# Turning the rows of routings 1 to 5 through DRAM and VectorE instead of TensorE

## The chip, the cores and the metric

The kernel runs on one core of a Trainium2 chip. The metric is the device time of one execution in microseconds (us). A core has these engines, each with its own in-order instruction queue: PE (TensorE, matrix products and transposes by an identity matrix, into PSUM), DVE (VectorE), ACT (ScalarE), POOL (GpSimd) and SP (SyncE, which here only issues transfers). Transfers run on 16 DMA engines. An engine waits at the head of its own queue until what it needs is there, and all that stands behind it waits too.

## The reference, cut to what matters

```python
x = x + scan_layer(layernorm(x), ...)            # "attn_a": 8 batches, 512 tokens, 256 features
x = x + ffn(layernorm(x), ...)                   # 16 routed experts, 4 per token, and 2 shared ones
x = x + attention(layernorm(x), ...)             # "attn_b"
x = x + ffn(layernorm(x), ...)

# in ffn, for each token row x of the normalised input:
scores = sigmoid(x @ router_w.T)                 # 16 experts
s = scores + bias
group_score = top_k(s by groups of 4, 2).sum()   # 4 groups, the best 2 are kept
topk_idx = top_k(masked s, 4)
tw = 2.5 * scores[topk_idx] / sum(scores[topk_idx])
routed = sum over the 4 chosen experts of tw * (silu(x @ gate) * (x @ up)) @ down
shared = (silu(x @ sh_gate) * (x @ sh_up)) @ sh_down
```

For the products with the router and the shared experts' weights, the 512 normalised rows of a batch (tokens on the partitions) have to be turned, so that the features lie on the partitions. This turning is what the change is about.

## The kernel before, in words

All arithmetic is in float32. Tokens are handled in 8 batches of 512. The program has four stages: the scan stage (scan layer of all batches, routing of the first mixture and its shared experts), the blocks of 128 tokens sorted by expert (the first mixture's routed experts), the attention stage with the routing and the shared experts of the second mixture, and the second mixture's blocks. The change touches the scan stage, which ends near 330 us.

`stretch(layer)` writes a stage. Its loop over the batch `b` makes one list of pieces of work for each turn and issues them beside each other: in the turn of batch `b` there are the scan of batch `b` (`main`: the products `pz_s` at L563, the scan itself on DVE, the output product `py_s` at L510), the normalisation of batch `b+1` with its turning (`xn`, `pt_l`) and the load of that batch's `x` (L149), the routing of batch `b-1` (class `Route`), and a share of the shared experts' work of earlier batches (`pg_m` at L1146, `pd_m` at L1174). `timed(steps, *places)` gives each step of a piece its place as a fraction of the turn. A scheduler then orders the instructions of each engine by these places and by what they need, and the order stays fixed in each engine's queue.

The routing of a batch has these steps. `norm` writes the normalised rows `sorted_m` on DVE (L493) at the places `norms`. `scores` turns them, then multiplies with the router (`logits`: 8 small products `pl_m`, L669), turns the small result on DVE (L680) and takes the sigmoid on ACT. `choices` picks the experts on DVE (L695 to L739); the product `pr_m` (L747) counts places early in the next turn; the rows are then scattered to DRAM by POOL (L798).

There are two ways to turn. `turned` (from L416) makes 8 PE transposes of 128x128 into two PSUM banks (L430) and two copies of 128x512 out of them (L432). For the routings of batches 0 to 5 in the scan stage both copies are ACT's and go into a place kept free in `w_all` (`kept_rows`), from which the shared experts read later. `by_shares` (from L435) stores the rows in DRAM (L440, 512 KB), loads them back in four shares of 128 KB, each of runs of 64 floats (L443), and then turns 32x32 blocks by two DVE transposes of 128x512 (L452). Before the change it is used in the attention stage only: `r.scores(i == 1)` at L1543.

What sets the order on the SP queue: in each turn the store of `x` of the batch before (L1444), then the load of the next `x` (L149), and directly behind it, by `Scan.load`, the loads of two experts' weights (in the turns of batches 2 to 5 six of 256 KB, L235 to L237) and one block of zeros (L348 or L351). The pool for `x` has three buffers, so the load of the next `x` waits until DVE has written the `sorted_m` rows that are read from the buffer to be reused. The stores of the shared experts' sums (`ys_m`, L1184) are also on SP. The tag `kb4` is a ring of 9 buffers of 512 KB, which also holds `xn`, the scan's `y_s`, the shared experts' `act_m` and `ys_m`.

Of the kernel before, what the change touches and what calls it, by code (L numbers as in the profile page):

```python
# [19 lines left out]
NT = T // P  # L20
# [62 lines left out]
def tile_hybrid_block(  # L83
# [276 lines left out]
    def behind(*pieces):  # L360
        def steps():
            for piece in pieces:
                yield from piece.steps

        return Piece(sum(piece.columns for piece in pieces), steps())

    def beside(*pieces):


        def steps():  # L370
            done = dict.fromkeys(range(len(pieces)), 0)
            while done:
                k = min(done, key=lambda k: done[k] / pieces[k].columns)
                step = next(pieces[k].steps, None)
                if step is None:
                    del done[k]
                else:
                    done[k] += step
                    yield step

        return Piece(sum(piece.columns for piece in pieces), steps())

    def timed(steps, *places):


        def scaled():
            now = 0
            for place in places:
                yield place - now
                now = place  # L390
                next(steps)
            for _ in steps:
                pass

        return Piece(1, scaled())

    def spread(first: float, last: float, many: int):
        return [first + (last - first) * k / many for k in range(many)]

    def some(steps, many: int):  # L400

        for _ in range(many):
            yield next(steps)

    def issue(piece):
        for _ in piece.steps:
            pass
# [114 lines left out]
    class Scan:  # L522
# [3 lines left out]
        early = 0  # L526


        norms, scores, choose = (0.08, 0.2, 0.32, 0.4), (0.53, 0.57, 0.65, 0.69), (0.71, 0.97)
        last_rows, last_scores = (0.26, 0.33), (0.43, 0.46)  # L530

        def load(self, b: int):
# [667 lines left out]
    class Attention:  # L1200
# [4 lines left out]
        norms, scores, choose = (0.0, 0.12, 0.2, 0.28), (0.29, 0.45, 0.55, 0.6), (0.66, 0.95)  # L1205
# [215 lines left out]
    def stretch(layer):  # L1421


        i = layer.mixture
        xT, xn, made, routes, sends = {}, {}, {}, {}, []

        def norm(b: int, first: bool = False):
            def place():
                xn[b] = kb4(f"xn_{i}_{b}")
                return xn[b]  # L1430

            return normed(b, f"l{i}_{b}", place, False, first)

        def turn(b: int, copies=layer.copies):
            if i == 1 and b >= layer.ahead:
                return by_shares(lambda: xn.pop(b), f"l{i}_{b}", lambda xnT: xT.update({b: xnT}), True)
            return turned(lambda: xn.pop(b), f"l{i}_{b}", lambda xnT: xT.update({b: xnT}), copies)

        def project(b: int):
            made[b], piece = layer.project(b, xT.pop(b))  # L1440
            return piece
# [12 lines left out]
        def experts(many: int):  # L1454
            return Piece(many * each, some(whole, many))
# [39 lines left out]
        def start_route(b: int):  # L1495
            routes[b] = Route(i, b, layer.copies)
            store(b)
            return routes[b]
# [4 lines left out]
        for b in range(1 if begun else 0, B):  # L1503
            pieces = [begun or layer.main(b, made.pop(b))]
            begun = None
            nxt, last = b + layer.ahead, b == B - 1
            scores, choose, turns = layer.scores, layer.choose, layer.turns
            if i == 0 and b == 1:

                scores, choose, turns = (0.95, 0.955, 0.97, 0.975), (0.98, 0.99), (0.96, 0.965)  # L1510
            fill = []
            if layer.ahead > 1 and not last:
                fill.append(project(b + 1))
            if b > 1:
                shared_sum = experts(layer.quota[last])
                fill.append(shared_sum)
                if len(sends) > 1:
                    pieces.append(timed(sends.pop(0), *spread(0.0, 0.16, layer.over)))
                wait = 0.16 if i == 0 and b == 2 else 0.0
                first = [wait + place for place in (0.1, 0.14, 0.18)]  # L1520
                if layer.over:
                    pieces.append(timed(some(sends[0], 3 + NT * TK - layer.over), *first, *spread(0.22 + wait, 0.97, NT * TK - layer.over)))
                else:
                    pieces.append(timed(sends.pop(), *first, *spread(0.22, 0.66 if last else 0.86, NT * TK)))
            if fill:
                pieces.append(behind(*fill))
            if b > 0:
                r = start_route(b - 1)
                if last:
                    pieces.append(timed(r.norm(), *spread(0.0, 0.12, NT), *spread(*layer.last_rows, NT)))  # L1530
                else:
                    first, then, rows, full = layer.norms
                    pieces.append(timed(r.norm(), *spread(first, then, NT), *spread(rows, full, NT)))
                sends.append(r.rest)
                if last:
                    pieces += [
                        timed(r.scores(), *layer.last_scores, *spread(0.5, 0.56, NT)),
                        timed(some(r.rest, PICKS), *spread(0.57, 0.67, PICKS - 1), 0.76),
                        timed(some(r.rest, 3 + layer.sent), 0.79, 0.81, 0.83, *spread(0.85, 1.0, layer.sent)),
                    ]  # L1540
                else:
                    pieces += [
                        timed(r.scores(i == 1), *scores[:2], *spread(*scores[2:], NT)),  # L1543
                        timed(some(r.rest, PICKS), *spread(*choose, PICKS)),
                    ]
            if nxt < B:
                added = layer.load(nxt)
                if added is not None:
                    pieces.append(timed(added, 0.31, 0.34))
                stats = 0.36 if added is not None else 0.32  # L1550
                pieces += [
                    timed(norm(nxt), *spread(stats, 0.44, NT), *spread(0.56, 0.64, NT)),
                    timed(turn(nxt), *turns),
                ]
            issue(beside(*pieces))
            if layer.ahead == 1 and nxt < B:
                issue(project(nxt))
            if i == 0 and b == 2:
                for make in pending:
                    make()  # L1560
# [4 lines left out]
        r = start_route(B - 1)  # L1565
# [24 lines left out]
    with banks_of(one=8):  # L1590
        table = stretch(Scan())
        wqkv_sb, wo_sb = load_attention_weights()
# [6 lines left out]
    with banks_of(one=4, pair=2):  # L1599
        table = stretch(Attention())  # L1600
# [87 lines left out]
```

## Time and profile before

| what | value |
|---|---|
| median of 13 runs | 1616.82 us (1613.52 to 1619.73) |
| the profiled execution: its own time | 1614.3 us |
| its span, first to last instruction | 1612.6 us |
| PE busy, share of the span | 1569.6 us (97%) |
| DVE, ACT, POOL busy | 1002.7, 780.1, 772.8 us |
| mean granted PE clock | 0.99 of full speed |
| turns of batches 2, 3, 4, 5, 6 in the scan stage start at | 49.7, 88.2, 122.2, 156.3, 190.4 us |
| the turn of batch 7 starts at | 226.1 us |
| a PE transpose `pt_m`, and an ACT copy out of it | 282 ns and 591 ns (medians) |
| a DVE transpose of `by_shares` (attention stage) | 700 ns (median of 12) |

A turn starts with the first `pz_s` product of its batch. The times of PE instructions overlap, since matmuls are pipelined: the step from one start to the next is what a group costs. So the 8 transposes `pt_m` at 105.80 are shown as 1.10 us, but the next product starts 0.94 us after them.

The views used are the page, the timelines of single engines (start, duration, engine, line, operation, output and inputs, count, and in brackets the idle time before it and what ended it), and tables by window of time (start:end, length, then busy time and count of PE, PE's weight loads, DVE, ACT and POOL, then the granted PE clock, the busy share of the DMA engines and GB/s). "SPq" is the SP queue issuing transfers.

### The profile page before, as it was taken

To read this page: it belongs to the slowest core of one execution; us is meant where nothing else is said; L and a number is where in the kernel's file an instruction comes from. 1 tells how busy PE (TensorE), PEld (TensorE's weight loads), DVE (VectorE), ACT (ScalarE), POOL (GpSimd) and SP (SyncE) were. 2 spreads that over 40 slices of the span, in tenths; PEclk is the share of its full clock that TensorE was granted. 3 is DMA by queue.
4 is the path that set the end of the run, shared out by engine and by line. 5 is a ranking of instruction groups with operands and counts; after the bars stand their busy time and mean duration, and the time that the engine had idled before them with its cause. 6 is when DMAs were issued, how large, how long until landed. Compare 5 with 4: busy or idle time off the path is not lost. (4 is left out here: it accounts for less than half of the span.)

```text
span 1612.6 us, 34092 instructions
## 1 busy us (share of the span) xinstructions
PE 1569.6 (97%) x10030; PEld 1158.2 (72%) x10030; DVE 1002.7 (62%) x3264; ACT 780.1 (48%) x1622; POOL 772.8 (48%) x639
## 2 busy tenths in 40 slices
PE   8999999999999999999999999999999999999996
PEld 6566666589999999983444454544558999999996
DVE  6887765344467444437888988878744444544453
ACT  3344443245555555546544554454224555555553
POOL 4376665535556555550014432433533555555554
PEclk9999999999999999999999999999999999999998
DMA  5454424557777666641323433343745767777776
GB/s 172 138 193 153 147 101 142 174 98 104 124 124 109 100 100 96 91 68 41 87 82 101 140 97 116 101 123 99 276 147 93 107 114 127 118 138 134 136 136 135
DMA packets 282765, 196.88 MB, mean 122 GB/s; under 512 B 168688, under 2 KB 262672, under 8 KB 282576
## 3 DMA queue, kind: packets, MB, share of 16 engines
q1 hardware_dynamic: 230016, 121.50, 28.8%
q0 software_dynamic: 51984, 72.09, 24.8%
q8 instruction: 85, 1.39, 0.4%
q10 hardware_dynamic: 576, 1.05, 0.2%
q14 instruction: 104, 0.85, 0.2%
HBM read 91.29 MB, written 103.23 MB: 121 GB/s over the span
## 5 line engine op out<-in xcount | busy, mean ns | idle before, releaser
L1073 POOL DMA_INDIRECT part<-rows x272 | 426.6, 1568 | 341.3 <-ACT rows L1072 251.8
L798 POOL DMA_INDIRECT xg<-sorted_m,slots_m x256 | 269.1, 1051 | 244.7 <-ACT slots_m L795 119.2
L1033 PEld LDWEIGHTS ph<-rows,gate 128*128 128x128 f32 x2160 | 277.6, 191 | 32.7 <-ACT rows L1016 22.6
L1033 PE MATMUL ph<-rows,gate 128*128 128x128 f32 x2160 | 291.7, 278 | 0.5 <-ACT rows L1016 0.5
L1033 PE MATMUL ph<-rows,up 128*128 128x128 f32 x2160 | 285.3, 275 | 0.0
L1063 PE MATMUL pyr<-w_all,rows 128*128 x1088 | 279.5, 380 | 1.4 <-DVE rows L1043 1.4
L1033 PEld LDWEIGHTS ph<-rows,up 128*128 128x128 f32 x2160 | 262.9, 192 | 0.0
L1006 DVE COPY up<-w_all 128x512 f32 x270 | 119.2, 442 | 226.3 <-PE ph L1033 211.5
L1006 ACT COPY gate<-w_all 128x512 f32 x270 | 166.4, 617 | 123.9 <-PE ph L1033 120.0
L1043 DVE TENSOR_TENSOR rows<-ph,rows 128x256 f32<-128x256 f32 x272 | 115.5, 425 | 155.8 <-PE ph L1033 141.9
L1295 ACT ACTIVATE w_all<-ps_a 128x1024 f32<-128x1024 f32 x160 | 155.2, 1021 | 107.0 <-PE ps_a L1285 102.2
L1063 PEld LDWEIGHTS pyr<-w_all,rows 128*128 128x128 f32 x1088 | 186.8, 192 | 15.8 <-DVE rows L1043 1.6
L1072 ACT ACTIVATE rows<-pyr,gain 128x256 f32<-128x256 f32 x272 | 128.9, 474 | 78.5 <-PE pyr L1063 61.7
L1041 ACT ACTIVATE rows<-ph 128x256 f32<-128x256 f32 x272 | 104.6, 384 | 117.0 <-PE ph L1033 106.7
L1174 PE MATMUL pd_m<-sd_sb,act_m 128*128 128x256 f32 x512 | 120.1, 384 | 2.2 <-DVE act_m L1165 1.3
L1174 PEld LDWEIGHTS pd_m<-sd_sb,act_m 128*128 128x128 f32 x512 | 96.3, 191 | 26.6 <-issue 9.0
L1285 PE MATMUL ps_a<-w_all 32*128 32x384 f32 (+3 forms) x1024 | 103.5, 470 | 9.8 <-ACT w_all L1295 9.7
L1305 DVE SCALAR_TENSOR_TENSOR w_all<-w_all,causal 128x512 f32<-128x512 f32 (+1 forms) x160 | 91.9, 574 | 27.9 <-ACT w_all L1295 26.8
L1146 PE MATMUL pg_m<-w_all,su_sb 128*128 128x512 f32 x192 | 92.7, 606 | 0.0
L1146 PE MATMUL pg_m<-w_all,sg_sb 128*128 128x512 f32 x192 | 92.2, 601 | 0.0
L1285 PEld LDWEIGHTS ps_a<-w_all 32*128 32x128 f32 x1024 | 44.9, 186 | 65.0 <-ACT w_all L1295 36.4
L1321 PE MATMUL po_a<-w_all,v_a 128*32 128x512 f32 (+3 forms) x1024 | 90.0, 449 | 0.0
(222 smaller groups left out, 1918.4 us busy)
## 6 DMA issues: line engine op xcount, KB each, us to landing
rows<-xg SPq DMA_DIRECT2D x720, 32.0 KB
rows<-xg SPq DMA_DIRECT2D x92, 134.0 KB
part<-x SPq DMA_DIRECT2D x16, 512.0 KB
w_all<-in_L_ffn_gate_w_dram SPq DMA_DIRECT2D x29, 256.0 KB
w_all<-in_L_ffn_up_w_dram SPq DMA_DIRECT2D x29, 256.0 KB
w_all<-in_L_ffn_down_w_dram SPq DMA_DIRECT2D x29, 256.0 KB
part<-ys_m SPq DMA_DIRECT2D x14, 512.0 KB
sum<-part SPq DMA_DIRECT2D x14, 512.0 KB
```

The costliest lines, as they stand in the source:

```text
L798: nc.gpsimd.indirect_dma_start(out=xg[i], out_offset=bass.IndirectOffsetOnAxis(ap=slots[:, at : at + 1], axis=0), in_=rows[:, t, :], in_of ...
L1006: copy(here, w_all[:, bass.ds(held[n][0] + half * KD * F, KD * F)])
L1033: nc.tensor.matmul(ph[s][:, f * P : (f + 1) * P], lhsT=both[s][:, k * F + f * P : k * F + (f + 1) * P], rhs=rows[:, ROW + k * P : ROW + (k ...
L1041: nc.scalar.activation(act, ph[0], AF.Silu)
L1043: made = nc.vector.tensor_mul(act, ph[1], act)
L1063: nc.tensor.matmul(py, lhsT=act[:, f * P : (f + 1) * P], rhs=w_all[:, bass.ds(w + 2 * KD * F + f * D, D)], start=(f == 0), stop=(f == KF - 1),
L1072: nc.scalar.mul(y, py, gain[:, TK : TK + 1])
L1073: acc = nc.gpsimd.indirect_dma_start(out=parts[i][n % 2], out_offset=bass.IndirectOffsetOnAxis(ap=rows[:, D + 2 * TK : D + 2 * TK + 1].bit ...
L1146: made = nc.tensor.matmul(dst, lhsT=w[:, k, f * P : (f + 1) * P], rhs=xnT[:, k, :], start=(k == 0), stop=(k == KD - 1),)
L1174: nc.tensor.matmul(py[:, j, :], lhsT=acts[n][:, f, t * P : (t + 1) * P], rhs=shared[n][3][:, f, :], start=(n == 0 and f == 0), stop=(n == ...
L1285: nc.tensor.matmul(ps[j // 2][:, j % 2, col : col + n], lhsT=k_sb[w][r, o, c * P : (c + 1) * P], rhs=q_sb[r, o, c * P : T], start=True, st ...
L1295: nc.scalar.activation(es[two], ps[two], AF.Exp, scale=ATT_SCALE)
```

## The change

The routings of batches 1 to 5 in the scan stage use `by_shares` instead of `turned`; batch 0 and the last two keep `turned`. (In the loop, `b` is the batch of the scan, and the routing is that of batch `b-1`; the turn `b = 7` has a call of its own.) The places of the routing steps in these turns move as well: the first step of `scores` (the store and the four loads) to 0.42 of the turn, the second (the DVE transposes) to 0.64, the router's product to 0.69 to 0.73, and the choice of the experts from 0.71 to 0.97 to 0.75 to 0.98.

```diff
-        norms, scores, choose = (0.08, 0.2, 0.32, 0.4), (0.53, 0.57, 0.65, 0.69), (0.71, 0.97)
+        norms, scores, choose = (0.08, 0.2, 0.32, 0.4), (0.42, 0.64, 0.69, 0.73), (0.75, 0.98)
...
-                        timed(r.scores(i == 1), *scores[:2], *spread(*scores[2:], NT)),
+                        timed(r.scores(i == 1 or b > 1), *scores[:2], *spread(*scores[2:], NT)),
```

The function that these routings now go through:

```python
    def by_shares(src, tag, into, into_rows, home=None):
        rows = src()
        through = dram.tile([T, D], FP, name=f"through_{tag}")
        nc.sync.dma_start(out=through.rearrange("(t p) d -> p t d", p=P), in_=rows)
        share = rows.rearrange("p t d -> p (t d)") if into_rows else kb4(f"share_{tag}").rearrange("p t d -> p (t d)")
        for a in range(QUAD):
            nc.sync.dma_start(
                out=share[a * SQ : (a + 1) * SQ, :].rearrange("s (g c) -> s g c", g=T // SQ),
                in_=through[:, a * KD * SQ : (a + 1) * KD * SQ].rearrange("(g s) c -> s g c", s=SQ),
            )
        yield 0
        dst = home() if home else work.tile([P, KD, T], FP, tag="kb4", name=f"xT_{tag}", bufs=KB)
        into(dst)
        for half in range(2):
            g = slice(half * T // SQ // 2, (half + 1) * T // SQ // 2)
            nc.vector.transpose(
                dst.rearrange("p k (g s) -> p k g s", s=SQ)[:, :, g],
                share.rearrange("p (g i k) -> p k g i", i=SQ, k=KD)[:, :, g],
            )
        yield 0
```

In the instruction lists of the built changed kernel, the 40 transposes `pt_m` of these batches and their 10 ACT copies are gone; SP has 25 more transfers and DVE 10 more transposes.

## The prediction

> **What bounds the kernel now.** I first looked at which engine has no idle time in the turns that the change touches. This is the table by windows, here the turn of batch 3:
>
> ```profile
> 88.20:122.20 34.00, 34.00 (x133) 20.85 (x132) 26.23 (x107) 15.14 (x37) 24.97 (x25) 1.00 0.52 174
> ```
>
> PE is busy in 34.00 of 34.00 us, at full clock (1.00). The turns of batches 4 and 5 read the same (34.10 of 34.10). So time taken off PE is gained here, and every microsecond that PE waits is lost: no later idle time could take it up. Next, PE's own timeline around the place of the edit:
>
> ```profile
> 105.80 1.10 PE L430 MATMUL pt_m<-ident,sorted_m 128*128 128x128 f32 x8
> 106.74 1.89 PE L510 MATMUL py_s<-w_scan,y_s 128*128 128x256 f32 x8
> 108.47 1.88 PE L1146 MATMUL pg_m<-w_all,sg_sb 128*128 128x512 f32 x4
> 110.28 0.64 PE L669 MATMUL pl_m<-w_all,rw_sb 128*32 128x128 f32 x16
> 110.85 1.99 PE L510 MATMUL py_s<-w_scan,y_s 128*128 128x256 f32 x8
> ```
>
> The 8 transposes cost 106.74 - 105.80 = 0.94 us, a group of `py_s` or `pg_m` 1.73. `pl_m` is what needs the turned rows. Then SP's timeline in the same turn:
>
> ```profile
> 102.88 0.37 SPq L149 DMA_DIRECT2D x<-in_L_attn_a_x_dram  x1
> 103.30 0.54 SPq L235 DMA_DIRECT2D w_all<-in_L_ffn_gate_w_dram  x1
> ...
> 105.88 0.62 SPq L237 DMA_DIRECT2D w_all<-in_L_ffn_down_w_dram  x1
> 106.54 0.51 SPq L351 DMA_DIRECT2D part<-zeros  x1
> ```
>
> The load of `x` is held until the `sorted_m` rows are written (DVE ends them at 102.86). So at the very moment at which the rows could be stored, 512 KB of `x`, six times 256 KB of weights and 128 KB of zeros enter the queue. How long they take, by windows (the last two numbers are the DMA engines' busy share and GB/s):
>
> ```profile
> 102.00:103.00 1.00, 1.00 (x4) 0.51 (x3) 1.00 (x4) 0.28 (x4) 0.73 (x1) 1.00 0.00 0
> ...
> 111.00:112.00 1.00, 1.00 (x5) 0.90 (x6) 0.30 (x1) 1.00 (x1) 0.83 (x3) 1.00 1.10 403
> 112.00:113.00 1.00, 1.00 (x5) 0.77 (x5) 0.12 (x1) 0.61 (x3) 0.85 (x1) 1.00 0.48 184
> ```
>
> The DMA engines are full until about 112.5. Last, what the same detour takes in the attention stage, from SP's timeline, the windows and DVE's timeline:
>
> ```profile
> 758.54 0.36 SPq L440 DMA_DIRECT2D through_l<-xn  x1
> 761.59 1.92 SPq L443 DMA_DIRECT2D xn<-through_l  x4
> ...
> 785.71 1.92 SPq L443 DMA_DIRECT2D share_m<-through_m  x4
> ```
>
> ```profile
> 786.50:789.50 3.00, 2.98 (x33) 1.26 (x25) 2.29 (x6) 2.12 (x3) 0.00 (x0) 1.00 1.03 174
> 789.50:790.50 1.00, 1.00 (x19) 0.38 (x17) 0.96 (x3) 1.00 (x2) 0.00 (x0) 1.00 0.03 3
> ```
>
> ```profile
> 791.07 1.31 DVE L452 STREAM_TRANSPOSE w_all<-share_m 128x512 f32<-128x512 f32 x2
> ```
>
> A store with an empty queue holds SP for 761.59 - 758.54 = 3.05 us. Its bytes move for about 1.4 us of that (512 KB at 350 to 370 GB/s) and end near 761.0, so the loads follow 0.6 us after the last byte. From the first share load to the last byte it takes 789.5 - 785.71 = 3.8 us (lower end). DVE used the rows at 791.07 without waiting, so they were there 5.4 us after the first load (upper end). The two transposes take 1.31.
>
> **What the change does, part by part.** *Removed:* 8 PE transposes in each of five turns, 5 x 0.94 = 4.7 us on the path; two ACT copies of 0.59 in each, worth nothing by themselves (ACT is busy 15.1 of 34.0 us), also not by the PSUM banks they free, since PE waited for no bank here.
>
> *Moved:* in the changed kernel's lists PE runs `py_s`, `pg_m`, `py_s`, then `pl_m`. In turn 3 `pl_m` is thus due at 105.80 + 3 x 1.73 = 111.0, and behind it lie 122.23 - 110.28 - 1.73 = 10.2 us of the turn (before, one `py_s` stood behind it). The choice of experts follows `pl_m` on DVE for some 10 us and is needed by `pr_m` about 15 us after it (5.2 us into the next turn), so its later places cost nothing as long as these 5 us last.
>
> *Added on SP:* in turns 2 to 5 the list has the store behind `x`, the six weights and the zeros, then the four loads, the first of which waits for the store to have landed. SP stands there; behind it are the store of the next `x` (needs DVE's sum at 121.8), then the next `x` (needs the next `sorted_m`): both later anyway, so this block of SP costs nothing. Turn 3 then: transfers ahead end 112.5, the store's bytes 113.9, loads 114.5, rows 118.3 to 119.9, turned 119.6 to 121.2, end of turn 129.8 to 131.4 instead of 122.23: **+7.6 to +9.2**, the 0.94 already credited. Turn 4: the engines are full until 149.0 (here also the `ys_m` store, which is ahead in the list too); by the same steps turned at 156.1 to 157.7, end 166.3 to 167.9 for 156.33: **+10.0 to +11.6**. Turn 5: full until 182.5, of which `ys_m`'s 1.4 now come behind the store; turned 188.2 to 189.8, end 198.4 to 200.0 for 190.42: **+8.0 to +9.6**. Turn 2: `x` was issued at 74.62 and the engines were full until 85.3; DVE's list now has 1.5 us of other work (0.68 + 0.41 + 0.38) behind the rows instead of ahead of them, so 83.8, loads 85.8, turned 90.9 to 92.5, plus the 10.2 left, end 101.1 to 102.7 for 88.16: **+13.0 to +14.6**.
>
> *Added on DVE:* two transposes a turn. In the list they stand behind the sum of the scan's first half (L519, which needs the `py_s` just ahead of `pl_m`), four rows of `xn` and six statistics: by DVE's rows 0.61 + 1.3 + 6 x 0.34 + 0.5 = 4.5 us. In turn 3 DVE comes to them at 111.2 + 4.5 = 115.7: earlier than the rows (118.3), so it is covered in turns 2 to 5 and is the bound if the rows come sooner. In turn 6 there is no `x` load and the store goes ahead of the two weight loads (SP, 203.94 and 204.80); the rows end at 204.95, so with 9 us (3.05 + 5.4) they are there near 214. There DVE decides: `py_s` ends 214.8, sum and two statistics 1.7, transposes 1.3, 217.8 against `pl_m` due at 216.5: +1.3 - 0.94 = **+0.4** (low end -0.9, if DVE's list is quicker).
>
> *Buffer:* a share takes one `kb4` slot a turn, so each tile inherits one released a little later; `y_s` now waits for a `ys_m` store, which was issued a turn (30 us) earlier. Nothing, as long as that cover stays.
>
> *Clock:* PE's speed after a wait is to be seen in these rows:
>
> ```profile
> 271.09 2.41 PE L430 MATMUL pt_m<-ident,sorted_m 128*128 128x128 f32 x8 [1.53 <-DVE sorted_m L493]
> 273.30 2.99 PE L1146 MATMUL pg_m<-w_all,su_sb 128*128 128x512 f32 x4
> ```
>
> After 1.53 us idle the granted clock fell to 0.50 from 272.2 to 275.7; the groups took 2.21 and 2.92 instead of 0.94 and 1.77: 2.4 us lost. The longest such stretch (46.8 to 53.5 at 0.50) lost half of 6.7, 3.4 us; after 1.65 us idle at 73.98 nothing was lost. Four waits of 8 us and more: 0 to 13.4; I take the nearest row, 4 x 2.4 = 9.7.
>
> The Trainium skill, "TensorE: Matmul & The Clock Gate", Part 1, says that the array runs at half clock until it has been busy for one window of about 3.4 us. By that each restart would lose about 1.7 us, an estimate from the page, and the sum would be 6.8 in place of 9.7.
>
> **Sum:** middles 13.8 + 8.4 + 10.8 + 8.8 + 0.4 = 42.2 (37.7 to 45.4), clock 9.7 (0 to 13.4): +51.9, from the profiled 1614.3 us to 1666.2. That execution is 2.5 us below the median of the runs; for the median I say 1668. Own range: 1616.8 + 37.7 = 1654 to 1616.8 + 45.4 + 13.4 = 1676.
>
> **Rivals.** (1) *The store overtakes the queue*, so that only its issue (107.1 in turn 3, behind the other issues) and 8.4 us of detour count. For it: SP is free to issue then. Against it: `x`, first in line, had landed 3.4 us after its issue in turn 5 (the issue at L236, held for it, ended at 174.28; issue at 170.89) although four more loads had been issued by then, so the engines serve in order. Turned then about 117 in turn 3 (DVE's list and the detour give nearly the same): +5.0, +8.5, +5.4, +4.9, +0.4 for turns 3, 2, 4, 5, 6, with the clock 34: 1651.
>
> (2) *The detour is hidden and the change gains* its 4.7 us: 1612. It decides if the turned rows are there by 111.0 in turn 3, so the loaded ones 6.8 us after `sorted_m`. For it: the attention stage hides the same detour, and its parts at their shortest make 3.05 + 3.8 = 6.9. Against it: 2.2 MB ahead in the queue, and DVE's 4.5 us between `py_s` and the transposes, which alone make 5 us of wait.
>
> (3) *The wait is longer than costed*: the scatters of POOL (0.37 of the DMA engines after 113) slow the loads, and the late choice of experts, with 5 us to spare, delays `pr_m`: another 3 us a turn, 1680.
>
> **Chances.** Forecast 0.71, rival 1 0.14, rival 2 0.06, rival 3 0.09. The range leaves out rival 2 and the far ends of 1 and 3: 1640 to 1682. A difference under 0.2% (3.2 us) can't be told from none: faster 0.04, same 0.02 (both from rival 2), slower 0.94.
>
> **What would show it.** In the changed trace: in turns 2 to 5 PE idle for 8 to 18 us right ahead of `pl_m`, released by DVE's L452, which was itself idle for the share loads; SP's L443 some 11 us after `x` was issued; PE's clock at 0.50 after each of these waits; turns of about 54, 45, 47, 45 us, and turn 6 at its old length. If L452 runs without waiting for a DMA, rival 1 or DVE's list is right; if `pl_m` doesn't wait at all, the forecast is wrong at its root.

## The result and the profile after

The changed kernel takes 1668.99 us (median of 8 runs, 1667.34 to 1670.62), the kernel before, on the same chips, 1616.71 us (median of 37 runs, 1611.88 to 1619.73). The ratio is 1.0325, with a 95% interval of 1.0315 to 1.0335: 52 us more. The profiled execution of the changed kernel took 1671.7 us, with a span of 1670.0 us and a mean granted PE clock of 0.974 (0.99 before). That execution is 2.7 us above its median and the one of before 2.5 us below its own, so the two profiles differ by 57.4 us where the medians differ by 52.3. What is read from the profiles below is to be compared with 57.4.

The table by windows of the changed kernel (window, length, then busy time of PE, PE's weight loads, DVE, ACT and POOL with counts, granted PE clock, DMA share, GB/s), one line for each of the turns of batches 2 to 6 (the last line runs 1.2 us into the turn of batch 7):

```profile
50.80:105.10 54.30, 35.41 (x129) 20.69 (x126) 35.93 (x137) 15.65 (x33) 16.57 (x19) 0.84 0.44 146
105.10:151.70 46.60, 35.78 (x126) 21.14 (x125) 28.36 (x108) 14.15 (x35) 22.68 (x23) 0.85 0.45 141
151.70:200.00 48.30, 35.34 (x134) 22.24 (x133) 28.20 (x90) 13.48 (x34) 22.69 (x23) 0.86 0.41 136
200.00:247.10 47.10, 35.52 (x133) 22.59 (x132) 26.36 (x88) 13.68 (x34) 22.50 (x23) 0.86 0.43 139
247.10:284.00 36.90, 34.87 (x136) 21.95 (x135) 26.23 (x85) 13.67 (x34) 23.24 (x24) 1.00 0.42 136
```

Before, PE was busy in 34.00 of the 34.00 us of turn 3. Now it is busy in 35.78 of 46.60, and the clock column has fallen from 1.00 to 0.85. By the first `pz_s` of each turn (50.82, 105.06, 151.66, 199.99, 247.31, 282.84) the turns are longer by 15.8, 12.5, 14.2, 13.2 and -0.1 us: 55.6 of the 57.4. Another 1.15 us come ahead of turn 2. Behind turn 6 nothing of note is left. The kernel before started turn 2 at half clock: its first `pz_s` and `pg_m` took 5.50 us together (49.67 to 55.17), where the changed kernel's took 3.54 (50.82 to 54.36). So about 2 us of the old turn 2 went to the clock, which the new one does not lose.

PE's timeline in turn 3 of the changed kernel shows where it goes:

```profile
124.42 1.88 PE L1146 MATMUL pg_m<-w_all,sg_sb 128*128 128x512 f32 x4
126.14 1.89 PE L510 MATMUL py_s<-w_scan,y_s 128*128 128x256 f32 x8
138.85 1.08 PE L669 MATMUL pl_m<-w_all,rw_sb 128*32 128x128 f32 x16 [10.82 <-DVE w_all L452]
139.86 3.78 PE L1146 MATMUL pg_m<-w_all,su_sb 128*128 128x512 f32 x4
143.44 1.50 PE L430 MATMUL pt_l<-ident,xn 128*128 128x128 f32 x8
144.77 1.89 PE L510 MATMUL py_s<-w_scan,y_s 128*128 128x256 f32 x8
```

PE stands 10.82 us ahead of `pl_m`, released by DVE's transposes. Behind the wait the next groups are slow: `pg_m` 3.58 us from start to start in place of 1.72 (124.42 to 126.14), `pl_m` 1.01 in place of 0.57. The other turns have the same line with 17.46, 12.96 and 11.59 us; turn 6 has 1.36. Now the transposes of the same turn in DVE's timeline, behind the sum of the scan's first half:

```profile
128.07 0.69 DVE L519 TENSOR_TENSOR x<-py_s,x 128x512 f32<-128x512 f32 x1 [4.41 <-PE py_s L510]
...
132.19 0.30 DVE L469 BATCH_NORM_AGGREGATE mv_l<-stats_l 128x2 f32<-128x6 f32 x2
137.40 1.30 DVE L452 STREAM_TRANSPOSE w_all<-share_m 128x512 f32<-128x512 f32 x2 [4.90 <-DMA share_m<-through_m]
```

DVE was through with its list at 132.5 and then stood 4.90 us for the share loads. And SP's timeline, with the reason:

```profile
119.78 0.37 SPq L149 DMA_DIRECT2D x<-in_L_attn_a_x_dram  x1
...
124.08 0.38 SPq L440 DMA_DIRECT2D through_m<-sorted_m  x1
132.40 1.92 SPq L443 DMA_DIRECT2D share_m<-through_m  x4
```

The store is issued 4.3 us after `x`, behind the weights, and the share loads 8.3 us after the store, which with an empty queue takes 3.05. The same stretch by windows:

```profile
128.00:131.00 3.00, 0.03 (x1) 0.00 (x0) 2.93 (x9) 0.32 (x1) 2.38 (x4) 0.95 1.08 397
131.00:138.00 7.00, 0.00 (x0) 0.00 (x0) 2.10 (x10) 0.00 (x0) 2.65 (x4) 0.50 0.60 144
138.00:139.00 1.00, 0.15 (x4) 0.18 (x8) 0.70 (x2) 0.00 (x0) 0.00 (x0) 0.50 0.00 0
139.00:144.00 5.00, 5.00 (x23) 2.44 (x20) 2.16 (x12) 0.26 (x1) 0.00 (x0) 0.50 0.00 2
145.00:151.00 6.00, 6.00 (x23) 4.17 (x22) 3.73 (x21) 2.73 (x7) 2.90 (x3) 1.00 0.15 55
```

The DMA engines are full (1.08, 397 GB/s) while PE already waits, and then only the shares move. The granted clock is 0.50 from 131 to 144 us: through the wait and for 5 us of work behind it. From 145 on it is 1.00 again.

### The profile page after: what moved, and what is told of

The parts are those of the page before. It is cut to its first block, busy times and chain, and to the rows that moved or that the text cites. A ratio compares the mean times of both kernels' runs of the same rounds, so it can differ in the third digit from the quotient of the medians.

```text
span 1670.0 us, 34054 instructions
## 1 busy us (share of the span) xinstructions
PE 1570.8 (94%) x9990; PEld 1155.9 (69%) x9990; DVE 1012.6 (61%) x3274; ACT 775.2 (46%) x1612; POOL 770.4 (46%) x639
## 5 line engine op out<-in xcount | busy, mean ns | idle before, releaser
L1063 PEld LDWEIGHTS pyr<-w_all,rows 128*128 128x128 f32 x1088 | 186.8, 192 | 15.8 <-DVE rows L1043 1.6
L1285 PE MATMUL ps_a<-w_all 32*128 32x384 f32 (+3 forms) x1024 | 103.4, 466 | 9.8 <-ACT w_all L1295 9.7
L1146 PE MATMUL pg_m<-w_all,su_sb 128*128 128x512 f32 x192 | 99.4, 643 | 0.0
```

What stands on the lines that cost most here:

```text
L1063: nc.tensor.matmul(py, lhsT=act[:, f * P : (f + 1) * P], rhs=w_all[:, bass.ds(w + 2 * KD * F + f * D, D)], start=(f == 0), stop=(f == KF - 1),
L1146: made = nc.tensor.matmul(dst, lhsT=w[:, k, f * P : (f + 1) * P], rhs=xnT[:, k, :], start=(k == 0), stop=(k == KD - 1),)
L1285: nc.tensor.matmul(ps[j // 2][:, j % 2, col : col + n], lhsT=k_sb[w][r, o, c * P : (c + 1) * P], rhs=q_sb[r, o, c * P : T], start=True, st ...
```

## The experiments

The theory is the prediction's: the transfers ahead of the store in SP's queue set the wait in turns 2 to 5, and the clock adds to it. Against it stand DVE's list, the length of the detour itself, and the mere traffic. The first four runs shared a chip on which the kernel before took 1617.2 us.

**Store first.** The load of `x` and the weight loads of turns 2 to 5 are kept back until the share loads are issued.

```diff
+                def loads():
+                    with tc.issue_after(load_x(b + 1).ins):
+                        for load in later[b - 1 :: shares]:
+                            load()
...
+                if b < 3:
+                    loads()
+                else:
+                    held_back.append(loads)
...
         for a in range(QUAD):
-            nc.sync.dma_start(
+            last = nc.sync.dma_start(
...
+        if held_back:
+            with tc.issue_after(last.ins):
+                held_back.pop(0)()
         yield 0
```

> The load of x and the weight loads of turns 2 to 5 are queued behind the share loads instead of ahead of the store. The forecast (the transfers ahead in SP's queue set the wait): the store follows the rows at once, the loads 3.05 us later, the rows land some 8.4 us after sorted_m (turn 3: 119.75 + 8.4 = 128.2 instead of 137.4). DVE's list then decides in turns 3 to 5 (sum, two statistics, transposes: 3.3 us behind py_s), so the waits ahead of pl_m fall from 17.5, 10.8, 13.0, 11.6 to about 8.5, 3.3, 3.3, 3.3 us: 34 us less, 1635 us (1630 to 1642). Rival 1 alone (DVE's list decides; here it loses xn and four statistics ahead of the transposes, 2.6 us a turn in three turns): 1661. Rival that it is the detour itself, whatever is ahead of it: 1669, L443 still 11 us after the rows.

Measured: 1636.8 us, ratio 1.0121 (1.0104 to 1.0138). The waits ahead of `pl_m` in turns 2 to 5 are 8.38, 3.18, 3.41 and 3.18 us, each within 0.2 of what was expected. Turn 3 in SP's timeline of this run, then in DVE's:

```profile
111.42 0.36 SPq L440 DMA_DIRECT2D through_m<-sorted_m  x1
114.42 2.08 SPq L443 DMA_DIRECT2D share_m<-through_m  x4
116.60 0.51 SPq L149 DMA_DIRECT2D x<-in_L_attn_a_x_dram  x1
```

```profile
119.58 0.69 DVE L522 TENSOR_TENSOR x<-py_s,x 128x512 f32<-128x512 f32 x1 [3.62 <-PE py_s L513]
...
121.27 1.30 DVE L455 STREAM_TRANSPOSE w_all<-share_m 128x512 f32<-128x512 f32 x2
```

The loads now follow the store by 3.00 us, and in turns 3 and 5 the transposes run without an idle time ahead of them (0.23 us in turn 4): DVE's list decides there. In turn 2 DVE still stands 4.72 us for the share loads. The edit gives back 1.0325 - 1.0121, 2.0% or 33 us of the 52. Some 8 of these (2.6 us in each of three turns, the expectation's own term) could be had only because four `xn` and some statistics had moved from ahead of the transposes in this run's DVE list as well.

**Transposes first.** In DVE's list the two transposes stand ahead of the sum of the scan's first half: their place in the turn is 0.48 in place of 0.64, and the sum is issued behind the last of them, which is kept in `turned_last`. SP's queue is unchanged.

```diff
-            nc.vector.transpose(
+            turned_last[:] = [nc.vector.transpose(
...
-            nc.vector.tensor_add(rows, py, rows)
+            with tc.issue_after(turned_last.pop().ins) if half == 0 and turned_last and "s" in tag else nullcontext():
+                nc.vector.tensor_add(rows, py, rows)
...
-        norms, scores, choose = (0.08, 0.2, 0.32, 0.4), (0.42, 0.64, 0.69, 0.73), (0.75, 0.98)
+        norms, scores, choose = (0.08, 0.2, 0.32, 0.4), (0.42, 0.48, 0.69, 0.73), (0.75, 0.98)
```

> The two transposes of DVE stand ahead of the sum of the scan's first half and of the statistics in DVE's list; SP's queue is as in the changed kernel. The forecast: they then wait for the same loads, so pl_m runs when it did; 1669 us (1665 to 1673), DVE L452 idle for the share loads 3 to 5 us longer than the 4.9 us of turn 3. Rival 1 (DVE's list decides): the 4.5 us of list ahead of the transposes are gained in turns 3, 4, 5, and 6: 1651.

Measured: 1668.4 us, ratio 1.0310 (1.0286 to 1.0334). DVE's timeline in turn 3:

```profile
137.14 1.30 DVE L454 STREAM_TRANSPOSE w_all<-share_m 128x512 f32<-128x512 f32 x2 [12.02 <-DMA share_m<-through_m]
```

DVE comes to the transposes 7 us earlier and waits 7 us longer (3 to 5 us had been expected), and `pl_m` is not earlier for it. Rival 1, in which its list decides, falls for the changed kernel. In turn 6, where PE does not stand for a load, the edit does gain: 34.1 us in place of 35.5.

**Both edits.**

> Both edits: the store ahead of x and the weights, the transposes ahead of the sum and the statistics. The forecast: the rows land 8.4 us after sorted_m and are turned 1.3 us later, so the waits are about 8.5 (turn 2), 1.7, 1.4 and 1.3 us: 40 us less than the changed kernel, and the clock stays up behind waits this short in part (0 to 7 us): 1629 us (1620 to 1633). If the half clock costs 2.4 us behind every wait however short: 1629. If nothing of the queue matters (rival 1 alone): 1651, as for the transposes alone.

Measured: 1631.3 us, ratio 1.0082 (1.0065 to 1.0098), so DVE's list is worth another 0.4% (6 us) once the queue is out of the way. Waits: 8.30, 1.54, 3.89 and 2.44 us. Turn 4 has 2.5 us more than expected, since there the store of `ys_m` came between the store and the share loads (issued at 150.32 and 151.12). Turn 5 has 1.1 us more: its rows came 6.4 us after the issue of the first share load (190.44 to 196.83), where turn 3 took 5.3 (116.07 to 121.36); why is open. Behind 1.54 and 2.44 us of waiting `pl_m` took 0.65 and 0.64 us, at full clock; behind 3.89 it took 1.08. Turn 2 is the plain price of the detour: its rows are ready (75.29) only 2 us ahead of the place of `pl_m` (77.46), and with an empty queue and the list out of the way 8.3 us remain.

**The traffic alone.** The kernel before, PE still turning, with a store and share loads that nobody reads.

```diff
+    def through_only(r, tag: str):
+        rows = r.held["rows"][:, :, 0:D]
+        through = dram.tile([T, D], FP, name=f"through_{tag}")
+        nc.sync.dma_start(out=through.rearrange("(t p) d -> p t d", p=P), in_=rows)
...
+                        *([timed(through_only(r, r.tag), 0.42)] if i == 0 and b > 1 else []),
                         timed(r.scores(i == 1), *scores[:2], *spread(*scores[2:], NT)),
```

> The kernel before with PE's transposes, and besides the store and the four share loads of the routings of batches 1 to 5 in the same places of SP's queue, whose rows nobody reads: the transfers without the wait. The forecast (the wait is the cost, the transfers cost nothing by themselves): 1617 us (1614 to 1622). Rival (the transfers delay scatters, weights or x, and PE with them): a good part of the 52 us, 1630 or more.

Measured: 1624.7 us, ratio 1.0046 (1.0029 to 1.0063): a miss by 7.5 us. Turns 3 to 6 took 34.1, 34.1, 34.1 and 36.1 us, but turn 2 took 47.1 (38.5 before). PE's timeline there:

```profile
74.05 1.13 PE L430 MATMUL pt_m<-ident,sorted_m 128*128 128x128 f32 x4 [2.69 <-DVE sorted_m L505]
...
87.45 0.81 PE L430 MATMUL pt_l<-ident,xn 128*128 128x128 f32 x2 [4.37 <-DVE xn L505]
```

The rows `xn` of the next batch had moved behind the first steps of the choice of experts in DVE's list (86.99 us, before 71.61 to 74.52). So this was a list that had come out otherwise in turn 2, and the run was repeated without that turn (`b > 2`):

> The traffic alone once more, without turn 2: the kernel before with the unused store and share loads of the routings of batches 2 to 5 (turns 3 to 6), PE's list as before. The 7.5 us that the run with turn 2 cost are put down to that turn, where DVE's list came out otherwise (xn behind the choice of experts, PE idle 4.4 us for it) and which took 47.1 us in place of 38.5, while turns 3 to 6 took 34.1, 34.1, 34.1 and 36.1. If that is so: the time of before (ratio 0.999 to 1.002). If the transfers themselves cost it: again 0.3 to 0.5% more.

Measured: ratio 1.0022 (1.0006 to 1.0037), 1641.6 us beside 1638.1: just above the first forecast and below the second. PE's list was the same here; DVE's was not quite. Turn 4 took 36.9 us, with PE 1.70 us idle for `act_m`, and turn 6 36.6. In turns 3 to 6 the transfers, and what they did to DVE's order, are thus worth some 3.5 us (1 to 6 by the interval) of the 52; the two were not separated, and turn 2 was not measured by itself.

**The wait filled.** Idle matmuls on a constant keep PE busy through most of each wait. The edit also moves the router's place from 0.69 to 0.72 and ties `pl_m` behind the last idle matmul; the lines below are against the kernel before. From here on the kernel before took 1636 to 1638 us on the chips that the runs were made on, so ratios are compared.

```diff
+                if half == 0 and j == 1 and hook:
+                    with tc.issue_after(made.ins):
+                        keep_busy({'s2': 74, 's3': 46, 's4': 55, 's5': 49}[tag], f"wait_{tag}")
+                    next(hook.pop())
...
-        norms, scores, choose = (0.08, 0.2, 0.32, 0.4), (0.53, 0.57, 0.65, 0.69), (0.71, 0.97)
+        norms, scores, choose = (0.08, 0.2, 0.32, 0.4), (0.42, 0.64, 0.72, 0.73), (0.75, 0.98)
...
+                with tc.issue_after(waited[-1].ins) if i == 0 and 0 < b < 5 else nullcontext():
```

> The changed kernel with idle matmuls (74, 46, 55, 49 of 128x128 on a constant, some 0.23 us each) between py_s and pl_m in turns 2 to 5, so that PE is busy through most of each wait; everything else stays where it was. The forecast, whose clock term is 9.7 us (9.2 measured as the longer pl_m, pg_m and pt_l groups): these groups run at full speed, 1660 us (1657 to 1665). Rival (the groups behind a wait are slow for another reason than the idle time): 1669. If the idle matmuls outlast the wait: each us of it adds one.

Measured: 1685.2 us, ratio 1.0294 (1.0274 to 1.0315). As ratios, the 1660 us of the forecast are about 1.027 and the rival's 1669 about 1.032; the measured one lies between them, so the time settles nothing. To have something to read it against, the changed kernel was run again without an edit:

> The changed kernel once more, without an edit. The runs with filled waits and with the store on ACT's queue were compared with a kernel before of 1636 to 1638 us, 20 us above that of the first runs. If the surplus of the change is the same there, and the two runs are to be read against it: ratio 1.0315 to 1.0335, waits ahead of pl_m of 17.5, 10.8, 13.0, 11.6 us within 1 us each. If on such a chip the rows land later (the filled run had them 1.5 to 1.9 us later in turns 3 and 4): waits 1 to 2 us longer, ratio 1.034 to 1.038.

Measured: 1688.5 us, ratio 1.0295 (1.0269 to 1.0322); by the medians 51.1 us more than before, by the ratio 48. The ratio lies below the expected 1.0315 to 1.0335, though the intervals overlap. The waits are 17.40, 10.79, 12.96 and 10.56 us. Turns 2 to 4 of the filled run by windows, and its `pl_m` of turn 3 in PE's timeline:

```profile
50.90:105.20 54.30, 51.10 (x276) 36.74 (x273) 35.51 (x137) 15.65 (x33) 16.72 (x19) 1.00 0.44 147
105.20:150.80 45.60, 43.56 (x218) 30.46 (x218) 28.46 (x108) 14.15 (x35) 22.70 (x23) 1.00 0.45 144
150.80:198.80 48.00, 45.42 (x243) 33.89 (x242) 27.13 (x89) 13.48 (x34) 22.84 (x23) 1.00 0.42 137
```

```profile
128.06 10.43 PE L429 MATMUL idle_wait_s<-ones 128*128 128x128 f32 x92
140.53 0.64 PE L689 MATMUL pl_m<-w_all,rw_sb 128*32 128x128 f32 x16 [2.04 <-DVE w_all L467]
```

The clock stays at 1.00. From `pl_m` to the end of the turn it is now 10.23 to 10.25 us in each of turns 2 to 5, beside 12.56, 11.60, 11.71 and 12.90 in the unedited run: 7.8 us less, the clock term as these two traces show it. Against it stands that `pl_m` itself ran 1.1, 1.5, 1.9 and 1.0 us later after the start of its turn (5.5 us together), since the turned rows came later. In turn 2 the four share loads took SP 3.25 us to issue in place of 1.92, and the transposes began 1.0 us later in the turn. In turn 4 the shares' last bytes had moved by about 185.0 and DVE began to turn them at 187.16, beside about 185.3 and 186.4 in the unedited run; why is open. That leaves 7.8 - 5.5 = 2.3 us, which the two ratios, 1.0294 and 1.0295, can't show. So the clock term is read from the traces; no difference in time shows it.

**Turn 6 alone.** The changed kernel's program with the detour for the routing of batch 5 only; turns 1 to 5 have their old places and turn on PE, as in the kernel before.

```diff
+            if i == 0 and 1 <= b < 6:
+                scores, choose = ((0.95, 0.955, 0.97, 0.975), (0.98, 0.99)) if b == 1 else ((0.53, 0.57, 0.65, 0.69), (0.71, 0.97))
...
-                        timed(r.scores(i == 1 or b > 1), *scores[:2], *spread(*scores[2:], NT)),
+                        timed(r.scores(i == 1 or b > 5), *scores[:2], *spread(*scores[2:], NT)),
```

> The kernel before with the detour for the routing of batch 5 alone (turn 6, where nothing is queued ahead of the store); turns 2 to 5 turn on PE as before. The forecast has +0.4 us for this turn, the changed kernel showed -0.1: 1617 us (1615.5 to 1618.5), the same as before. Rival that the detour costs a wait of its own, whatever stands ahead of it: some 8 us, 1625.

Measured: ratio 1.0002 (0.9987 to 1.0018), turn 6 in 35.5 us. The interval leaves out the rival's 8 us, but can't tell the predicted +0.4 from the -0.1 of the changed kernel. Where nothing is queued ahead, the rows come in time and the change is neutral within about 3 us. Turns 2 and 3 took 40.3 and 35.8 us here, with PE turning and no detour in them; they took 40.8 and 35.9 in the run with the traffic in turns 3 to 6, so these two lengths are not the traffic's doing.

**Store on ACT's queue.**

```diff
-        nc.sync.dma_start(out=through.rearrange("(t p) d -> p t d", p=P), in_=rows)
+        (nc.sync if into_rows else nc.scalar).dma_start(out=through.rearrange("(t p) d -> p t d", p=P), in_=rows)
```

> The changed kernel with the store of the rows issued on ACT's queue; x, weights and share loads stay on SP's. If the DMA engines serve what was issued first, whatever the queue (as the forecast takes it), the store waits for the transfers ahead of it all the same: ratio 1.030 to 1.034, the share loads issued some 11 us after x. If each queue is served beside the others, the store lands within about 4 us of its issue, the loads are issued while the weights still move and stand behind them alone: rows 2 to 4 us a turn earlier, ratio 1.024 to 1.028.

Measured: 1684.7 us beside 1638.1, ratio 1.0295 (1.0272 to 1.0319). From ACT's and from SP's timeline in turn 4:

```profile
163.60 0.45 ACTq L440 DMA_DIRECT2D through_m<-sorted_m  x1
```

```profile
163.60 0.40 SPq L149 DMA_DIRECT2D x<-in_L_attn_a_x_dram  x1
...
168.71 0.33 SPq L351 DMA_DIRECT2D part<-zeros  x1
169.54 0.38 SPq L1184 DMA_DIRECT2D part<-ys_m  x1
170.06 5.95 SPq L443 DMA_DIRECT2D share_m<-through_m  x4
```

Behind the zeros SP stood 0.4 us for `through_m` and then went on with the store of `ys_m` at 169.54: the store of the rows had landed 5.9 us after it was issued (5.7 to 6.4 us in the four turns), although `x`, six weights and the zeros were issued on SP's queue at the same time and in the 5.1 us behind it. In the unedited run the share loads follow `x` by 14.9 us in this turn. The store did not stand behind the weights, then. But it had been issued at the same moment as `x` and ahead of the weights, so order of issue, whatever the queue, would bring it early as well: behind `x` alone it would land some 4.4 us after its issue (3.05 and 1.3 for `x`, an estimate from 512 KB at 397 GB/s), with `x` as in the unedited run. Both came later than that: the store by more than 1 us, and `x` in turn 2 after 5.1 us in place of 4.2. That speaks for two queues served side by side; a run with the store issued on ACT's queue behind the weights, which would show it, is missing. The expectation had 4 us for the store, and a ratio of 1.030 to 1.034 or of 1.024 to 1.028; the measured one lies between the two. The waits were 15.30, 8.99, 10.23 and 8.50 us, 1.8 to 2.7 us shorter than in the unedited run; that they are not shorter still is put down to the weights, behind which the share loads still stood in SP's queue, but no run with the store on ACT's queue had them elsewhere. The ratio is the same as that of the unedited run (1.0295), so that no gain in time is shown, where the waits add up to 8.7 us.

**Tries at a version that keeps PE's gain.** The detour in turns 3 to 6 only, with both edits, and `pl_m` later in PE's list (`Scan`'s places for the scores 0.78 and 0.82, and 0.85 and 0.88).

> A try at a version that keeps PE's gain: the detour in turns 3 to 6 alone (turn 2 turns on PE), store and share loads ahead of x and the weights, transposes ahead of the sum, and pl_m later by two pg_m and the first half of the pt_l groups (2.2 us). With the waits of the run that had both edits (1.5, 3.9 and 2.4 us in turns 3 to 5) that leaves 0, 1.7 and 0.2, against 0.94 gained a turn: turn 4 +0.8 to +3.2, the others -0.7 to -0.9: 1616 us (1613.5 to 1619). If a later pl_m makes pr_m late in the next turn, as rival 3 has it: 1620 or more.

> As the run with later logits, but pl_m behind the other pt_l and py_s groups and a pd_m, 8 to 10 us later than in the changed kernel's list: no wait ahead of pl_m is left, and the choice of experts has to fit in what was spared behind it. If its 5 us of slack and the places that were moved with it are enough: 1613 us (1611 to 1616). If pr_m becomes the wait (rival 3): 2 to 5 us a turn in three turns, 1620 to 1630.

Measured: ratio 1.0035 (1.0023 to 1.0047) for the first, some 6 us more than before, where the time of before had been forecast, and 1.0167 (1.0151 to 1.0182) for the second: 27 us, more than its forecast and its rival had. In the second PE waited for `sel_m` (0.91 and 1.70 us, turns 4 and 6) and `act_m` (4.63 us, turn 6): what rival 3 feared. It also still waited 3.09, 2.54 and 3.09 us ahead of `pl_m` in turns 4 to 6, where none had been expected. In the first the waits ahead of `pl_m` were 1.69, 1.73 and 1.69 us in turns 3 to 5, with no DMA named behind them. The turns took 39.0, 35.1, 34.9 and 34.2 us; turn 3 is the long one, since PE also stood 2.19 us for the scan's `y_s` there (110.80) and the clock then fell to 0.50 until about 115. The 1.73 us of turn 4, from DVE's timeline:

```profile
153.56 0.69 DVE L1179 TENSOR_TENSOR act_m<-pg_m,sig_m 128x512 f32<-128x512 f32 x1 [4.91 <-PE pt_l L430]
154.20 1.31 DVE L457 STREAM_TRANSPOSE w_all<-share_m 128x512 f32<-128x512 f32 x2
```

`act_m` needs the `pg_m` that had been moved ahead of `pl_m` to cover the wait, and stood ahead of the transposes in DVE's list: the cover had become a part of the wait. It was put behind them:

```diff
-                        nc.vector.tensor_mul(act[:, f, :], pu, sig)
+                        with tc.issue_after(turned_last[-1].ins) if i == 0 and turned_last else nullcontext():
+                            nc.vector.tensor_mul(act[:, f, :], pu, sig)
```

> The run with later logits again (detour in turns 3 to 6), with act_m, which needs the pg_m just ahead of pl_m, put behind the transposes in DVE's list; it stood ahead of them and made the 1.7 us waits of turns 3 to 5. Without these waits: turns 3 and 5 gain up to 0.9 us each, turn 6 1.4 as seen, turn 4 (where the ys_m store goes ahead of the share loads) loses about 0.6: 2 to 3 us below before (ratio 0.998 to 0.999). If the rows land too late anyway: the ratio stays at 1.0035.

Measured: ratio 1.0028 (1.0011 to 1.0045), the same as without this edit; the forecast of 0.998 to 0.999 is missed. Turn 3 in DVE's timeline, then in PE's:

```profile
118.19 1.30 DVE L457 STREAM_TRANSPOSE w_all<-share_m 128x512 f32<-128x512 f32 x2 [4.59 <-DMA share_m<-through_m]
```

```profile
119.64 0.64 PE L683 MATMUL pl_m<-w_all,rw_sb 128*32 128x128 f32 x16 [1.55 <-ACT xT_l L432]
```

With `act_m` out of the way the transposes stood for the share loads themselves: 4.59, 4.97 and 5.50 us in turns 3 to 5, with the rows 6.1 to 6.9 us after the first load's issue. `pl_m` followed the end of the transposes by 0.15 us in each of the three turns. (In turns 3 and 5 the profile puts its wait, 1.55 and 0.62 us, down to ACT's copy `xT_l`; in turn 3 that copy had ended at 118.71.) So the rows landed too late anyway, the expectation's second case. No version tried here beats the kernel before.

## Why the prediction was right

*PE without slack.* Right: the turns grew by what PE waited and by what its clock lost, and no later idle time took any of it up.

*The queue ahead of the store.* Right, and shown by removing it: 33 of 52 us went (some 8 of them with the help of a shorter DVE list), and the waits fell to the values worked out for an empty queue and that list. In turn 3 the terms were 11.6 us from the issue of `x` to that of the share loads (114.5 - 102.88), 3.8 to 5.4 to the rows, and 1.31. Measured: 12.62 (132.40 - 119.78), 5.0 (137.40 - 132.40), and 1.30 with 0.15 to PE. The 1.0 us in the first is the mis-sized one: the engines stayed full until about 132, 12.2 us behind the issue of `x`, where the store's last byte had been costed at 11.0. Without the clock, the turns were predicted at +13.8, +8.4, +10.8, +8.8 and +0.4. The profile has 15.8, 12.5, 14.2, 13.2 and -0.1, of which 1.65, 2.7, 2.3 and 2.6 are the clock: +14.1, +9.8, +11.9, +10.6 and -0.1, or 46.3 in place of 42.2. Turns 3 to 5 lie above the middles by 1.4, 1.1 and 1.8 us, beyond the upper ends by 0.3 to 1.0. Turn 2 is better read by its end, since its terms were counted from the issue of `x` (74.62 before, 74.56 after), and the old turn's half clock lies ahead of that: without the clock it ends at 105.06 - 1.65 = 103.4, where 101.1 to 102.7 had been worked out, 1.5 us above the middle. There the share loads were issued 12.7 us after `x` (74.56 to 87.28) in place of 11.2. So each of the four turns was undersized by 1.1 to 1.8 us, 5.8 together.

*Clock.* 9.7 us for four restarts; 9.2 by the longer groups of the changed kernel, 7.8 by the run with filled waits. Right in kind and near in size, in part by luck: the 2.4 us of the nearest row were a misreading. The window in which its first group began is at full clock, and PE stood still in a part of it:

```profile
271.00:272.00 1.00, 0.84 (x3) 0.56 (x3) 1.00 (x3) 0.00 (x0) 0.54 (x2) 1.00 0.12 43
```

The clock was at 0.50 from about 272.2 to 275.5, which by the prediction's own rule (half of the stretch) loses 1.7 us. In the changed kernel the half clock lasted longer: from the start of `pl_m` about 5 us in turn 3 (139 to 144 us), 4.5 in turn 4 and 5.3 in turn 5, but 3.3 in turn 2. The Trainium skill, "TensorE: Matmul & The Clock Gate", Part 1, made it 6.8, an estimate from its window of about 3.4 us; turn 2 agrees with that window (3.3 us, 1.65 lost), turns 3 to 5 do not (2.3 to 2.7 lost), so both measures of the sum lie above the page's.

*DVE's list, rival 1.* Covered as predicted, and the bound as soon as the queue is gone: 3.18 us of wait, where 4.5 us of list had been worked out, of which that run's order took 2.6 away, and 1.3 for the transposes (3.2). The argument against rival 1, "the engines serve in order", fits SP's own queue, where the store behind `x` and the weights held the share loads for 8.3 us; whether it holds between two queues the run with ACT's did not settle. Its row for `x` is not borne out, however: SP's waits between 165 and 180 us show none for `x` at L236. Such a wait stands at L236 at 49.39 us of the kernel before, 4.1 us after the issue of `x`, and in turn 2 of the changed kernel `x` was there 4.4 us after its issue. That rival 1 falls rests on the runs, then, and not on that row.

*Turn 6.* +0.4 predicted with a low end of -0.9; -0.1, and no difference by itself.

*Buffer, ACT copies, the later choice.* At nothing, as costed: the slack of 5 us ahead of `pr_m` was enough. It is not enough for a `pl_m` 8 to 10 us later.

*The sum.* 51.9 us predicted, 52.3 by the medians, 57.4 by the two profiles. The agreement with the medians is closer than the steps deserve: by the profiles, which the terms were made against, the queue was undersized by nearly 6 us, and the medians differ by 5 us less than the profiles do, which made up for it. That is luck.

## What to carry to other kernels

Price a store and reload by the place of the store in its queue, not by its bytes: in turn 3, 8.3 us from rows written to rows back (both edits, 113.08 to 121.36) were 17.6 behind loads that start at the same event (changed kernel, 119.78 to 137.40), and 19.8 in turn 4. Take the transfers that nobody waits for behind those that somebody waits for; here that one edit gave back 33 us, some 8 of them with a shorter DVE list. And before moving work off a full engine, look for what covers the new latency; here the rows were back too late in turns 3 to 5 even with two more groups as cover. Look also at what the cover feeds: `act_m`, fed by one of those groups, stood ahead of the awaited transposes on DVE. Moving it changed what the transposes waited for, and the time hardly (1.0035 and 1.0028).

## What the hardware showed that was not expected

- A 512 KB store on ACT's queue, issued at the same moment as `x` on SP's, had landed 5.9 us after its issue (5.7 to 6.4 in the four turns), while some 1.5 MB of weights were issued on SP's; behind `x` and the weights on SP's own queue the share loads were issued 14.9 us after `x`. That two queues are served side by side is likely from this, not shown.
- How long PE has waited does not alone decide its clock. It fell to 0.50 after 1.53 us (the kernel before, 271.09) and after 2.19 us (first later `pl_m`, turn 3), and stayed at full speed after 1.54 and 2.44 us (both edits). Where it falls, the first group can still be quick: behind 3.18 us (store first) `pl_m` took 1.08 us in turn 3 and 0.65 in turn 5, but in turn 5 the clock was at 0.50 a microsecond later (201 to 204 us), and `pg_m` took 3.29 us in place of 1.72.
- Between the last bytes of the shares and the start of DVE's transposes lay about 1.2 us in the unedited run and over 2 us in one turn of the filled one. This gap is part of the 5.0 us from load to rows, and its cause is open.
